# Gated graph network and graph convolution on one core: every turn of h between layers across DRAM, held transfers, and norms in three half-steps

## The chip, the cores and the metric

One core of a Trainium2 chip. A core has five engines, each with its own queue of instructions that it works off in order: PE (TensorE, matrix products into the accumulation banks called PSUM), DVE (VectorE), ACT (ScalarE), POOL (GpSimd), and SP (SyncE, which here only issues transfers). Transfers (DMA) between DRAM and the on-chip memory SBUF are issued from SP and POOL. The metric is the device time of one execution in microseconds (us); lower is better.

## The reference, cut to what matters

There are 16 graphs ("batches") of 1024 nodes with 128 channels. `adj` holds zeros and ones. Two blocks follow each other, each with a layer norm and a relu in front and a residual around it.

```
h = relu(layernorm(x))                       # block 0: gated graph network, 4 layers
for i in range(4):
    m = adj^T @ (h @ weight[i])              # per batch: 1024 x 1024 by 1024 x 128
    r = sigmoid(m @ Wr + h @ Ur + b);  z = sigmoid(m @ Wz + h @ Uz + b)
    n = tanh(m @ Wn + b + r * (h @ Un + b))
    h = (1 - z) * n + z * h
x = x + h * nodemask
h = relu(layernorm(x))                       # block 1: graph convolution, 4 layers
for i in range(4):
    h = relu(adj @ (h @ W[i]) + b[i])
    h = batch_norm over all 16 * 1024 nodes (gamma[i], beta[i])
out = x + h
```

## The kernel before, in words

`exact_path` does the work. Block 0 takes the batches two at a time: stream `sa` has the even batches, `sb` the odd ones. Everything in block 0 is in the layout "channels on the 128 partitions, nodes along the row", except what enters the product with `adj` (`aggregate_rows`, L525), which needs h with nodes on the partitions. So between two layers h has to be turned. The turned h is split into a high part (fp32r, ACT) and a low part (the rest, DVE): `ghw`, two tiles of 128x1024.

The turn is done in two ways. *Across DRAM*: DVE turns blocks of 32x32 (`half_out`, L704), SP stores the half (256 KB) to a scratch tensor `cross_h` (L591), four SP loads of 64 KB bring it back in the other order (`exchange_in`, L598, tile `n_h`), and `split_back` (L852 on ACT, L853 on DVE) makes `ghw`. *On PE*: `features_times` with no weights (L498), eight transposes into PSUM, then L502 on ACT and L503 on DVE. `turned_away` (L828) decides: across, except in the first two half-steps and except for `sb` ahead of its layer 3.

The order is written out in `half_step(one, two)`: the gates of `two` (`gate_step`, L916 on PE, then L928 to L943 on ACT and DVE, one half of 512 nodes after the other), then the product with `adj` of `one` (`agg_step`), for the layer that follows. The next half-step swaps them. A pair of batches takes eight half-steps. This text numbers them by what is multiplied with `adj`:

| step | product with adj | gates | also, before the change |
|---|---|---|---|
| 0 | sb layer 0 | sa layer 0 | `transposes` starts on the new pair |
| 1 | sa layer 1 | sb layer 0 | xmid of the old sa stored |
| 2 | sb layer 1 | sa layer 1 | ymid of the old sa, xmid of the old sb stored |
| 3 | sa layer 2 | sb layer 1 | start: ymid of the old sb, both x of the next pair loaded, adjT of sa stored |
| 4 | sb layer 2 | sa layer 2 | |
| 5 | sa layer 3 | sb layer 2 | start: adjT of sb stored; end: `fetch` for sa |
| 6 | sb layer 3 | sa layer 3 | h of sb turned on PE; rows of the next sa; end: `fetch` for sb |
| 7 | next sa layer 0 | sb layer 3 | rows of the next sb |

Beside this runs the preparation of other work:

- *adj for block 1* (`Feed`, `transposes`): POOL casts a row block to bf16 (L609), SP turns it by a transposing transfer (L610) into the one tile `adjT` (2 MB), and POOL stores that to `adjT_d` (L623). `feed.some(n)` takes n of the sixteen row blocks of a pair.
- *adj of the next batch*: `fetch` (L794) and `stage_rows` (L573) load eight row blocks of 512 KB, four at a time, into `stage`, which is the same memory as `adjT`. POOL rounds each to fp32r (`round_rows`, L578). Each is also looked at, to see that its values are exact: on ACT (`glance`, L587) for blocks 0 to 3, on DVE (`look`, L604) for 4 to 7. Then the next four may be loaded over them.
- *norms*: sums (L651, L652 on DVE), a root and factors (L655 on ACT, L658, L663 on DVE), eight normed blocks (L667 on ACT). Each root brings two table loads on ACT. `xmid_d` and `ymid_d` (512 KB each a batch) hold the residual and the normed input of block 1; POOL stores them. The x of the next pair is loaded by POOL as well (L540).

POOL and SP follow the written order. PE, DVE and ACT are put in order by a planner when the kernel is built, within the data dependences and the `behind(...)` edges, which say only "not ahead of this instruction of the same engine".

Block 1 (from L1177) multiplies again with `adj`, with the blocks loaded from `adjT_d`; the change does not touch it but for the name of one call.

Of the kernel before, what the change touches and what calls it, by code (L numbers as in the profile page):

```python
# [16 lines left out]
P = 128  # L17
# [324 lines left out]
def exact_path(  # L342
# [191 lines left out]
    with ExitStack() as st:  # L534
# [77 lines left out]
        def transposes(batches):  # L612

            for b, rows in batches:
                adjT = turned_tile(f"adjT{b}")
                ahead = transpose_rows(b, rows[0], 0, adjT)
                for j in range(NB):
                    go = ahead
                    if j + 1 < NB:
                        ahead = transpose_rows(b, rows[j + 1], j + 1, adjT)  # L620
                    go()
                    yield j
                nc.gpsimd.dma_start(adjT_d[b].rearrange("k p n -> p k n"), adjT)  # L623

        class Feed:
            jobs, open = iter(()), True

            def some(self, n):
                for _ in range(n):
                    if self.open and next(self.jobs, None) == NB - 1:  # L630
                        self.open = False

        feed, later = Feed(), []

        def soon(b, go):

            later.append(go) if b + 2 < B else go()

# [60 lines left out]
        def blocks_out(src, name):  # L699

            return [half_out(cross_tile(f"t_{name}_{hf}"), src, hf, name) for hf in range(NH)]

        def half_out(t, src, hf, name):
            nc.vector.transpose(by_nodes(t), four_ways(src[:, hf * HALF : (hf + 1) * HALF]))  # L704
            return exchange_out(t, f"{name}_{hf}")

        def cross_tile(name):
            return half_tile(name).bitcast(F32)

        def tail_norm(b, xt, hT, parts=None):  # L710

            for hf in range(NH):
                if parts:
                    pt = by_nodes(parts[hf])
                else:
                    pt = tmp(f"pt_x{b}_{hf}")
                    for q in range(BH):
                        k = hf * BH + q
                        nc.tensor.transpose(pt[:, q * P : (q + 1) * P], hT[:, k * P : (k + 1) * P], ident)
                    pt = four_ways(pt)  # L720
                for q in range(BH):
                    k = hf * BH + q
                    xk = xt[:, k, :].rearrange("p (a c) -> p a c", a=4)
                    mask = maskT[:, b * NB + k : b * NB + k + 1]
                    nc.vector.scalar_tensor_tensor(xk, pt[:, q, :, :], mask, xk, ALU.mult, ALU.add)
            nt = norm_stats(xt, f"mid{b}")
            if b + 1 < B:
                y = work.tile([P, N], F32, tag="h", name=f"y_mid{b}", bufs=7)
            else:
                y = xt.rearrange("p k c -> p (k c)")  # L730
            soon(b, lambda: nc.gpsimd.dma_start(xmid_d[b].rearrange("(k p) c -> p k c", p=P), xt))

            def rest():
                norm_apply(xt, y, nt)
                soon(b, lambda: nc.gpsimd.dma_start(ymid_d[b], y))

            return rest
# [10 lines left out]
        class Stream:  # L748


            def __init__(self, first):
                self.b, self.i, self.tag = first, 0, "AB"[first % 2]
                self.opened, self.across, self.ends, self.stage = None, False, [], None
                self.outs, self.split, self.started = [], [], False

# [32 lines left out]

            def prepare(self):
                self.next_y = work.tile([P, N], F32, tag=f"y{self.tag}", name=f"y_in{self.b + 2}", bufs=1)  # L790
                with behind(self.last_act):
                    norm_blocks(self.next_x, self.next_y, self.next_norm, range(NB))

            def fetch(self):  # L794

                if self.i == 3 and self.b + 2 < B:
                    stage = turned_tile(f"stage{self.b + 2}").bitcast(F32)
                    self.stage = [stage[:, 2 * q : 2 * q + 2, :].rearrange("p a n -> p (a n)") for q in range(4)]
                    stage_rows(self.b + 2, self.stage, range(4))

            def root_ahead(self):
                if self.i == 2 and self.b + 2 < B:
                    with behind(self.last_act):
                        norm_root(self.next_norm, 0, NB)
                        norm_scale(self.next_norm, 0, NB)

            def first_four(self):
                if self.stage:
                    with behind(self.first_act):
                        glance(self.b + 2, self.stage, range(4))  # L810
                    self.rows = round_rows(self.b + 2, self.stage, range(4))
                    stage_rows(self.b + 2, self.stage, range(4, NB))

            def last_four(self):
                if self.stage:
                    self.rows += round_rows(self.b + 2, self.stage, range(4, NB))
                    with behind(self.last_dve):
                        for j in range(4, NB):
                            look(self.b + 2, self.stage[j % 4], j)
                    self.stage = None  # L820

# [6 lines left out]
            def turned_away(self, i):  # L828

                return not written[0] and i < L and not (self is sb and i == 3)  # L830

            def half_away(self, hf):

                if self.turned_away(self.i + 1 - hf):
                    nm = f"{self.b}_{self.i + 1 - hf}"
                    self.outs.append(half_out(cross_tile(f"t_h{nm}_{hf}"), self.new, hf, f"h{nm}"))

# [109 lines left out]

            def ahead(self):

                if self.b + 2 >= B:  # L950
                    return
                if self.i == 2 and self is sa:
                    later.extend((sa.load_ahead, sb.load_ahead))
                if self.i == 3:
                    self.prepare()

            def finish(self):
# [4 lines left out]
                self.b, self.i = self.b + 2, 0  # L962
                ins = self.take() if self.b < B else None
                if not ins:
                    self.ends = [tail_norm(*args)]
                    return
                h_in = self.hT
                outs = blocks_out(args[-1], f"out{args[0]}")
# [7 lines left out]

                later.append(arrive)
                self.ends = [lambda: self.ends.append(lambda: self.ends.append(tail_norm(*args, parts)))]

            def end_step(self, *after):  # L980
                if self.ends:
                    with behind(*after):
                        self.ends.pop(0)()

            def sums_ahead(self, two):

                if self.i == 2 and self.b + 2 < B:
                    self.next_norm = norm_tiles(f"in{self.b + 2}")
                    with behind(two.last_dve):
                        norm_sums(self.next_x, self.next_norm, range(NB))  # L990

        def deliver():
            for go in later:
                go()
            later.clear()

        def half_step(one, two, gated=None, halfway=None):

            feed.open = True
            deliver()  # L1000
            if one is sb and one.i == 0 or not sb.started:
                feed.jobs, sb.started = transposes([(s.b, s.rows) for s in (sa, sb)]), True
            if one.i > 0:
                one.split_step()
            if one.i > 0:
                feed.some(2)
            two.gate_step(0)
            two.half_away(0)
            two.first_four()
            two.root_ahead()  # L1010
            one.split_back(0, two.last_act, two.last_dve)
# [3 lines left out]
            two.gate_step(1, None, one.split)  # L1015
            two.half_away(1)
            if one.i == 0:
                feed.some(1)
# [7 lines left out]
            if halfway:  # L1026
                halfway()
            one.end_step(two.last_act, *one.split)
            two.end_step(two.last_dve, *one.split)
            with behind(*one.split):  # L1030
                two.ahead()
            feed.some(1)
            with behind(*one.split):
                one.sums_ahead(two)
            one.agg_step(1)
            two.finish()
            one.fetch()

        sa, sb = Stream(0), Stream(1)
        every = {getattr(mybir.EngineType, e) for e in ("PE", "DVE", "Activation", "Pool", "SP")}  # L1040
        with tc.tile_pool(name="prep", bufs=1) as prep, tc.manual_schedule(engines=every):
# [101 lines left out]
            sb.agg_rows(range(4, NB))  # L1143
            sa.ahead()

            def looks():
                for j in range(4, NB):
                    first_look(1, j, raw1[j])

            half_step(sa, sb, looks, lambda: turn_layer(prep, w_g, 1))  # L1150
            join_layer(1)
# [4 lines left out]
        with tc.manual_schedule(engines={mybir.EngineType.Pool, mybir.EngineType.SP}):  # L1156
            written[0] = False
            for s in range(2, B // 2 * L):
                half_step(sa, sb)
                half_step(sb, sa)  # L1160
            deliver()
            sb.gate_step(0)
            sb.gate_step(1)
            with tc.issue_after(sb.last_act.ins):
                sa.ends.pop()()
            sb.finish()
# [164 lines left out]
    for b in range(B):  # L1331
# [4 lines left out]
        if waiting:  # L1336
            last = first_weights(*waiting, stats)
            if b == 1:
                with tc.issue_after(last.ins):
                    sb.ends.pop()()  # L1340
        if b == B - 1:
# [117 lines left out]
```

## Time and profile before

| what | us |
|---|---|
| median of 3 runs | 1822.87 |
| the three runs | 1816.81, 1822.87, 1825.02 |
| the profiled execution | 1826.22 |
| its span | 1824.3 |
| PE busy, share of the span | 1772.9, 97% |
| DVE, ACT, POOL busy | 1249.3, 1076.2, 364.4 |

The profile is one execution. The span is from its first to its last recorded instruction; the profiled execution is 1.9 us longer than its span and 3.35 us above the median. Block 0 takes about the first 1200 us of the span. PE's clock is at 9 tenths or more of full speed in all 40 slices.

### The profile page before, as it was taken

What the parts mean: (1) busy time and instruction counts of PE and PEld (TensorE: products, weight loads), DVE (VectorE), ACT (ScalarE), POOL (GpSimd) and SP (SyncE); (2) the same over time, 40 slices, a digit from 0 to 9 for tenths busy, and PEclk for the clock granted to TensorE, in tenths of its full rate; (3) what the DMA queues carried; (4) which work ended last, traced back from release to release, by engine and by line L of the source; (5) the groups of instructions that cost most, each with busy time, mean ns of one, the idle gap of its engine ahead of it and who ended that gap; (6) DMA issues with size and microseconds to landing.
All of it is one profiled execution on the core that took longest, in us unless ns stands there. A gap on an engine that the chain in (4) does not pass through costs nothing.

```text
span 1824.3 us, 22144 instructions
## 1 busy us (share of the span) xinstructions
PE 1772.9 (97%) x6806; PEld 1202.5 (66%) x6806; DVE 1249.3 (68%) x2319; ACT 1076.2 (59%) x1661; POOL 364.4 (20%) x378
## 2 busy tenths in 40 slices
PE   8999999999999999999999999999999999999997
PEld 5565655556555656565655555567778888888886
DVE  7667757767766866776776775676666666666665
ACT  5355546455457465555545545467677768768764
POOL 4223223322322332322232232010100000000010
PEclk9999999999999999999999999999999999999999
DMA  7366676775776677667586577678866666666666
GB/s 257 90 207 209 164 192 214 205 195 185 227 195 187 212 199 202 209 169 205 199 214 182 193 222 210 205 255 302 306 221 222 240 217 244 224 238 231 242 219 256
DMA packets 352447, 390.71 MB, mean 214 GB/s; under 512 B 158540, under 2 KB 231024, under 8 KB 352320
## 3 DMA queue, kind: packets, MB, share of 16 engines
q1 hardware_dynamic: 331568, 314.15, 56.1%
q0 software_dynamic: 20224, 74.80, 11.8%
q8 instruction: 55, 0.90, 0.2%
q14 instruction: 72, 0.59, 0.1%
q10 hardware_dynamic: 528, 0.26, 0.0%
HBM read 262.75 MB, written 92.80 MB: 195 GB/s over the span
## 4 chain that ended last, share of the span: by engine, by line
PE 63%; DVE 13%; DMA 9%; ACT 7%; SPq 4%; issue 4%; POOL 0%; DVEq 0%; ACTq 0%; POOLq 0%
PE pm L525 13%; PE pc_m L525 12%; PE g_r L916 6%; PE pc_g_r L525 6%; PE pc_g_z L525 6%; PE g_z L916 6%; PE hw_c L500 4%; DMA n_h<-cross_h 4%; PE g_xn L916 3%; SPq L598 3%; DVE h L943 2%; PE g_hn L916 2%; DVE low L604 2%; DVE h L942 2%; DMA cross_out<-t_out 1%
## 5 line engine op out<-in xcount | busy, mean ns | idle before, releaser
L525 PE MATMUL pm<-row,ghw 128*128 128x512 f32 x2048 | 514.9, 407 | 15.5 <-DVE ghw L853 15.5
L525 PEld LDWEIGHTS pm<-row,ghw 128*128 128x128 f32 x2048 | 387.0, 190 | 130.5 <-issue 29.7
L525 PE MATMUL pc_m<-wide,chw 128*128 128x512 f32 x1024 | 246.0, 395 | 0.0
L929 DVE SCALAR_TENSOR_TENSOR r<-g_hn,vecs,r 128x512 f32<-128x512 f32 x128 | 95.3, 745 | 180.0 <-ACT r L928 103.2
L525 PEld LDWEIGHTS pc_m<-wide,chw 128*128 128x128 f32 x1024 | 190.5, 188 | 42.3 <-issue 4.3
L609 POOL CAST half<-row 128x1024 bf16<-128x1024 f32 x128 | 138.3, 1090 | 311.0 <-DMA adjT<-half 296.8
L578 POOL CAST row<-stage 128x1024 fp32r<-128x1024 f32 x112 | 129.3, 1156 | 294.7 <-DMA stage<-in_adj_dram 213.1
L525 PE MATMUL pc_g_r<-wide,chw 128*128 128x512 f32 x464 | 187.0, 403 | 0.3 <-ACT chw L502 0.3
L525 PE MATMUL pc_g_z<-wide,chw 128*128 128x512 f32 x464 | 180.9, 390 | 0.0
L891 ACT COPY m<-pm 128x512 f32<-128x512 f32 x128 | 68.5, 587 | 188.7 <-PE pm L525 188.5
L934 ACT ACTIVATE r<-r,vecs 128x512 f32<-128x512 f32 x128 | 92.0, 719 | 145.5 <-DVE r L930 145.5
L1191 DVE CAST wide<-block 128x1024 fp32r<-128x1024 bf16 x160 | 109.9, 692 | 75.2 <-PE pc_m L525 40.0
L1191 DVE CAST wide<-packed 128x1024 fp32r<-128x1024 bf16 x160 | 110.3, 691 | 73.4 <-PE pc_g_z L525 54.2
L916 PE MATMUL g_r<-m,w_mT 128*128 128x512 f32 x256 | 131.5, 595 | 9.4 <-ACT m L891 9.4
L1189 ACT CAST wide<-packed 128x1024 fp32r<-128x1024 bf16 x96 | 100.6, 1048 | 59.3 <-PE pc_m L525 29.8
L935 ACT ACTIVATE z<-g_z,brz 128x512 f32<-128x512 f32 x128 | 86.9, 679 | 81.0 <-PE g_z L916 80.8
L1189 ACT CAST wide<-block 128x1024 fp32r<-128x1024 bf16 x96 | 100.7, 1049 | 57.2 <-PE pc_g_z L525 27.7
L916 PE MATMUL g_xn<-m,w_mT 128*128 128x512 f32 x256 | 130.7, 592 | 0.0
L916 PE MATMUL g_z<-m,w_mT 128*128 128x512 f32 x256 | 130.7, 592 | 0.0
L941 DVE TENSOR_TENSOR h<-h,r 128x512 f32<-128x512 f32 x96 | 75.3, 785 | 69.7 <-ACT r L934 69.6
L1239 DVE BATCH_NORM_STATS2 stats<-feat 128x6 f32<-128x512 f32 x128 | 84.1, 686 | 46.9 <-ACT feat L1238 45.8
L928 ACT ACTIVATE r<-g_r,brz 128x512 f32<-128x512 f32 x128 | 87.8, 686 | 43.7 <-PE g_r L916 43.3
(185 smaller groups left out, 2793.8 us busy)
## 6 DMA issues: line engine op xcount, KB each, us to landing
packed<-adjT_d SPq DMA_DIRECT2D x256, 256.0 KB, 5.7
block<-adjT_d SPq DMA_DIRECT2D x256, 256.0 KB, 4.6
stage<-in_adj_dram SPq DMA_DIRECT2D x120, 512.0 KB, 5.1
adjT_d<-adjT POOLq DMA_DIRECT2D x16, 2048.0 KB, 9.2
cross_h<-t_h SPq DMA_DIRECT2D x74, 256.0 KB, 2.3
n_h<-cross_h SPq DMA_DIRECT2D x296, 64.0 KB, 2.1
xmid_d<-x POOLq DMA_DIRECT2D x16, 512.0 KB, 5.1
y<-ymid_d POOLq DMA_DIRECT2D x16, 512.0 KB, 6.0
```

Of the source, the lines that this page charges most:

```text
L525: nc.tensor.matmul(pm[hf], hw[s][:, j * P : (j + 1) * P], rows[j][:, hf * HALF : (hf + 1) * HALF], start=(j == 0 and s == 0), stop=(j == N ...
L578: nc.gpsimd.tensor_copy(t, stage[j % 4])
L609: nc.gpsimd.tensor_copy(t, row.bitcast(F32))
L916: nc.tensor.matmul(po, wT[:, i, g * C : (g + 1) * C], rhs, start=start, stop=stop)
L928: self.first_act = nc.scalar.activation(r, pr, AF.Sigmoid, bias=brz[:, 3 * i : 3 * i + 1])
L929: nc.vector.scalar_tensor_tensor(r, phn, b_hn(i), r, ALU.add, ALU.mult)
L934: nc.scalar.activation(r, r, AF.Tanh, bias=b_in(i))
L935: self.last_act = nc.scalar.activation(z, pz, AF.Sigmoid, bias=brz[:, 3 * i + 1 : 3 * i + 2])
L941: nc.vector.tensor_sub(ho, hin, r)
L1189: nc.scalar.copy(r, t)
L1191: nc.vector.tensor_copy(r, t)
L1239: nc.vector.bn_stats(stats[:, b * NH + hf, :], dst)
```

## The change

1. `turned_away` no longer leaves out `sb` ahead of layer 3: eight turns go across DRAM that were done on PE. `self.last_dve` becomes the DVE turn of the half.
2. The large POOL transfers (adjT, xmid, ymid, x) are no longer issued at the start or end of a half-step. They are issued in its middle, on POOL behind a small copy `pace` that reads a column of the first half of the new h. adjT of sa goes out in step 2, that of sb in step 5. `x` of sa is loaded in step 3, of sb in step 4.
3. Each norm is spread over the ends ("gap") of three half-steps, written down in an agenda: sums, then root and factors, then blocks. Before, the root of the next pair's norm was taken between the two halves of the gates, and the norm of the finished pair was done in two places.
4. `fetch` moves from the end of a half-step to the start of the next; for sa it stands on SP behind the return of sb's h. Blocks 4 to 7 are loaded in `last_four`, not `first_four`. ACT looks at block 0 behind the first sigmoid of the first half of the gates, at 1 to 3 behind that of the second half. Blocks 4 to 7 of `sb` are looked at on ACT in step 0, no longer on DVE in step 7.
5. In the first half-step all eight row blocks of sa's `adjT` are turned.

```diff
+            def store(self):
+                if self.full and not self.stored:
+                    self.stored = next(self.jobs) == NB
...
-                return not written[0] and i < L and not (self is sb and i == 3)
+                return not written[0] and i < L
...
+                    at(n + 2, "gap", sums)
+                    at(n + 3, "mid", lambda: store_xmid(b, xt))
+                    at(n + 3, "gap", lambda: norm_factors(end["norm"]))
+                    at(n + 4, "gap", blocks)
+                    at(n + 5, "mid", lambda: store_ymid(b, end["y"]))
+                if self.b + 2 < B:
+                    at(n + 5, "mid", self.next_load)
+                    at(n + 5, "gap", self.next_sums)
+                    at(n + 6, "gap", self.next_factors)
+                    at(n + 7, "gap", self.next_blocks)
...
             def first_four(self):
                 if self.stage:
                     with behind(self.first_act):
-                        glance(self.b + 2, self.stage, range(4))
+                        glance(self.b + 2, self.stage, range(1))
                     self.rows = round_rows(self.b + 2, self.stage, range(4))
-                    stage_rows(self.b + 2, self.stage, range(4, NB))
 
             def last_four(self):
                 if self.stage:
+                    with behind(self.first_act):
+                        glance(self.b + 2, self.stage, range(1, 4))
+                    stage_rows(self.b + 2, self.stage, range(4, NB))
                     self.rows += round_rows(self.b + 2, self.stage, range(4, NB))
+                    b, stage, self.stage = self.b + 2, self.stage, None
+                    if self is sb:
+
+                        at(clock[0] + 1, "late", lambda: glance(b, stage, range(4, NB)))
+                        return
                     with behind(self.last_dve):
...
         def half_step(one, two, gated=None, halfway=None):
 
-            feed.open = True
-            deliver()
-            if one is sb and one.i == 0 or not sb.started:
-                feed.jobs, sb.started = transposes([(s.b, s.rows) for s in (sa, sb)]), True
+            feed.next_step()
+            one.split = []
+            if one.i == 0:
+                two.fetch()
+            due("ins")
+            if one is sb and one.i == 0 or written[0] and one is sa:
+                feed.jobs = transposes([(s.b, s.rows) for s in (sa, sb)])
             if one.i > 0:
                 one.split_step()
-            if one.i > 0:
+                two.fetch()
                 feed.some(2)
             two.gate_step(0)
             two.half_away(0)
             two.first_four()
-            two.root_ahead()
+            if feed.full or (clock[0], "mid") in agenda:
+
+                pace = small.tile([P, 1], F32, tag="pace", name=f"pace{clock[0]}")
+                nc.gpsimd.tensor_copy(pace, two.new[:, :1])
+                feed.store()
+                due("mid")
             one.split_back(0, two.last_act, two.last_dve)
             one.split_back(1, two.last_act, two.last_dve)
             if one.i > 0:
                 feed.some(1)
             two.gate_step(1, None, one.split)
             two.half_away(1)
+            with behind(two.first_act):
+                due("late")
...
-            one.end_step(two.last_act, *one.split)
-            two.end_step(two.last_dve, *one.split)
-            with behind(*one.split):
-                two.ahead()
-            feed.some(1)
-            with behind(*one.split):
-                one.sums_ahead(two)
+            with behind(two.last_act, two.last_dve, *one.split):
+                due("gap")
+            feed.some(NB if written[0] and one is sa else 1)
             one.agg_step(1)
             two.finish()
-            one.fetch()
+            clock[0] += 1
```

## The prediction

> **What bounds the kernel now.** I read the page first (is one engine full?), then PE's timeline for one pair of batches (where is it not?), then the chain of waits back from each gap.
>
> ```profile
> span 1824.3 us, 22144 instructions
> PE 1772.9 (97%) x6806; PEld 1202.5 (66%) x6806; DVE 1249.3 (68%) x2319; ACT 1076.2 (59%) x1661; POOL 364.4 (20%) x378
> ```
>
> PE is the bound. So a change can gain only what PE does needlessly, and PE's gaps. PE's timeline of one pair (start, us, engine, line, tiles; the bracket is the idle time ahead and what ended it):
>
> ```profile
> 684.42 7.11 PE L525 MATMUL pm<-row,ghw 128*128 128x512 f32 x30 [0.49 <-DVE ghw L853]
> ...
> 701.27 7.84 PE L525 MATMUL pm<-row,ghw 128*128 128x512 f32 x32
> ...
> 718.85 7.85 PE L525 MATMUL pm<-row,ghw 128*128 128x512 f32 x32
> 726.54 0.60 PE L498 MATMUL hw_g<-ident,h 128*128 128x128 f32 x4
> 728.28 0.66 PE L498 MATMUL hw_g<-ident,h 128*128 128x128 f32 x4 [1.15 <-DVE h L943]
> ...
> 755.83 1.12 PE L916 MATMUL g_z<-h,w_hhT 128*128 128x512 f32 x2 [0.73 <-ACT z L935]
> ...
> 804.47 1.12 PE L916 MATMUL g_r<-m,w_mT 128*128 128x512 f32 x2 [1.60 <-ACT m L891]
> ...
> 832.41 7.78 PE L525 MATMUL pm<-row,ghw 128*128 128x512 f32 x26 [1.88 <-DVE ghw L853]
> ```
>
> An undisturbed half-step is 718.85 - 701.27 = 17.58 us; eight are 140.64. This pair took 832.41 - 684.42 = 147.99. The same starts over seven pairs (129.62 to 1162.59 us) give 147.57 a pair, so 6.93 us a pair is lost. I split it by the steps in which it falls, averaged over the seven pairs: 2.31 in steps 6 and 7 (the turn on PE, its wait for h, a wait for a z bank), 1.36 in steps 0 and 1 (the wait for m), 3.26 in steps 2 and 3 (the wait for ghw). Removing all of it would be worth about 7 x 6.93 + 3 (the last pair's turn step, 20.62 us) = 52 us: no reading of this change ends below about 1771.
>
> The chain of waits behind the last gap, and POOL's timeline just ahead of it:
>
> ```profile
> 820.45 0.79 SPq L598
> 821.28 7.73 DMA n_h<-cross_h
> 829.20 0.48 issue
> 829.69 0.69 ACT r L928
> ...
> 831.07 0.68 DVE h L943
> 831.75 0.61 DVE ghw L853
> 832.41 2.76 PE pm L525 x6
> ```
>
> ```profile
> 819.28 0.56 POOL L735 DMA_DIRECT2D ymid_d<-y_mid  x1 [12.54 <-ACT y_mid L667]
> 819.84 1.77 POOL L540 DMA_DIRECT2D x<-in_x_dram  x2
> 821.60 0.89 POOL L623 DMA_DIRECT2D adjT_d<-adjT  x1
> ```
>
> The last 64 KB of the returning h took 7.73 us, where the page gives 2.1 as the median. POOL had issued 3.5 MB in the 3 us around it. ACT waits in its queue with the copy of that half; the sigmoid of the gates stands behind it, DVE behind the sigmoid, and DVE's low part of the *first* half, which PE wants, behind that.
>
> **The change part by part.**
>
> *The turn (part 1).* Eight turns leave PE: 8 transposes x 145 ns (12.8 us busy over 88) = 1.16 us each, 9.3 us, all on the path, as PE is the bound. Their copies (L502 0.60 and L503 0.69 us, twice) give way to L852 0.61 and L853 0.78, twice: nothing. Added for each turn: two DVE turns of 0.70 us, two stores and eight loads on SP (some 4.9 us of issue). When is it back? DVE's h is done at 728.24, and at about 726.8 without the doubled L942 and L943 of 1.41 us beside POOL's casts, which go elsewhere. Then 0.7 turn, 2.3 out, 1.7 issue, 2.1 back: 733.6; 1.4 for the split: 735.0. PE wants it at 726.5 + 10.3 (gates) = 736.8. So the cover is 1.8 us for the first four blocks, 3.6 more for the rest; without it, it costs what it is late. What was waiting around the turn (2.31 - 1.16 = 1.15 us a pair) I do not count as gained: the z bank is held up by DVE, where sa's four looks (4.5 us) stay, and the staged rows come later (below).
>
> *The held transfers (part 2).* The adjT store of sa leaves from the middle of step 2, at about 813.5 (first half of h at 812.5, `pace`, issue 0.89), with 0.5 MB of xmid; the profile's landings of 8.1 to 12.2 us put its end at 822 to 826. The returning second half is then in by about 825 and split by 827, wanted at 829.5 + 3.6. Ends late next: the planned order of DVE, some tenths. I count 2.4 of the 3.26 us a pair: 7 x 2.4 = 16.8 us. Queued behind `pace` on POOL, up to 9 us of a half-step: the stores and loads themselves and the casts of the last two row blocks (L609, 1.09 us each), whose transposing transfers on SP slip with them; adjT is wanted two half-steps on. The trace has no POOL copy of one column; by its DMA issues it is 0.5 to 0.9 us, or nearly nothing by its 128 elements, off the path in steps 1 to 5 either way. POOL is busy 20%.
>
> Here a rule of the Trainium skill speaks against the change. "DMA: Bandwidth & Descriptors", section "Queues, rings and completion order", says that each DMA engine goes round between the queues that have work, a packet at a time. Two busy queues (SP's, POOL's) would then slow a 2.1 us load to some 4.2 (an estimate from the page), and the half would land at 825.5, ahead of 829: no wait to remove, and the sum of the change would be the 9.3 of the turn alone. The trace has 7.73, and 6.68 at the other store (712.88 us, step 5). I take the measurement, 16.8, and keep the other as a rival. The rule also says that the bytes don't go away: the store now meets the *second* half's way out (817.2 us). At 8 us instead of 2.3 this comes back at about 829, still ahead of 833.1.
>
> *The norms (part 3).* The same instructions in other places. Two table loads and a root (1.28 + 0.30 + 1.28 us) leave the middle of ACT's gates and go behind them, where ACT waits for PE (188.5 us at L891). Sums of 8 x (0.26 + 0.16) = 3.4 us come in DVE's gap; x is issued some 8 us ahead of them and lands in 7.3. If it is late, DVE stands, and the next gate's r with it: up to 2 us in steps 3 and 4, which have no wait now; unlike it may gain the 1.36 us of steps 0 and 1. Bounds -9.5 to +10 us over the pairs; I take zero.
>
> *Rows and looks (part 4).* sa's fetch is issued at 719.86 now, when the store of sb's adjT (711.75) has landed. That store moves to about 717.1, landing at 726 to 728, and the fetch stands on SP behind the eight loads of h, whose last go at 731.6: 11.8 us later. But blocks 4 to 7 are now issued at 732.5 to 737.3 because ACT's looks and a busy row tile (735.89, wait for PE) hold them; with rows landing from 735 they go at 737 to 741.7, 4.4 later, land by 747, and DVE's looks end at 748.5, now 749.0. So it is just covered. For sb, four looks of 1.21 us leave DVE and 4 x (1.05 + 0.19) come to ACT in step 0, beside PE's 17.58. Zero, with a bound of +8 us a pair where the cover fails. Part 5: once, some 0.
>
> *Sum:* 9.3 + 16.8 = 26.1. The profiled execution's 1826.2 becomes 1800.1; it stood 3.4 above the median, so 1797.
>
> **The rivals.**
>
> *More goes than I count* (25%): the store at 711.75 also made h late for the turn (ACT waited for n_h until 719.66, then the table load, 721.59), so the 1.15 a pair around the turn goes too (9 us), and the steps 0 and 1 are planned anew (9.5): 1797 - 18.5 = 1778. For it: these waits hang on the same transfers. Against: sa's looks stay on DVE.
>
> *The hold only moves the collision* (14%): the second half or x is met instead. Only the turn remains: 1822.9 - 9.3 = 1813.5. For it: DMA is busy 68 to 69% throughout these stages.
>
> *Slower: the staged rows come late* (10%). Place: SP, the fetch behind the return of h, in step 6. If blocks 4 to 7 slip by 8 of the 11.8 us, sa's looks stand at the head of DVE's queue, sb's gates of step 7 (L929 at 751.87) behind them, and PE behind a bank. It has no slack there (0.73 us wait now), so about 7 us a pair: 49 - 26 = 23 slower, 1846. It decides from a slip of about 5 us, where the loss (some 4 us a pair) equals the 26 gained. Against: the 4.4 worked out above, which DVE's later end of looks absorbs.
>
> *It does nothing measurable* (3%): PE waits as long for h across as it spent on the turn, and the planner's order keeps the gaps: 1821.
>
> **How the numbers follow.** The case of the sum has 48%, 1788 to 1806. A measurement of this kernel can tell about 0.5% from no change: below 1813.8 is faster, above 1832.0 slower. Faster: 48 + 25 + half of 14 = 80%. Same: 7 + 3 + 1 (the mild end of late rows) = 11%. Slower: 9%. The range goes from 1773 (most of the second case) to 1822 (the third and the fifth); left out are the slower case and a tail of the second.
>
> **What would show it.** Right: 24 records of L498 `hw_g` instead of 88; `cross_h` issued 90 times, not 74; adjT_d issued in steps 2 and 5 beside a finished first half; no n_h landing of over 6 us on the chain in step 3; steps 2 and 3 together at 35.2 to 36; pairs at about 144. Wrong: gaps of PE behind `ghw` in step 6 (the turn is late), behind `row` in step 0 or 7, or `DMA stage` ended DVE or ACT waits of several us in steps 6 and 7 (the rows are late); or n_h landings over 6 us elsewhere (the collision moved).

## The result and the profile after

Over twelve runs of each, the changed kernel takes 1811.6 us (1809.0 to 1816.0) where the kernel before took 1828.0 (1816.8 to 1832.8): a ratio of 0.9915, with a 95% interval of 0.9897 to 0.9933, or 15.5 us (the medians lie 16.4 apart). The forecast was 26 us, and a time of 1797. Direction and range held; the runs below show that the sum behind them did not. One of its two terms had the wrong sign, and the other came out larger than forecast, partly in other steps.

The page after (span, then busy time of each engine):

```profile
span 1808.8 us, 22303 instructions
PE 1767.1 (98%) x6742; PEld 1192.1 (66%) x6742; DVE 1282.7 (71%) x2307; ACT 1106.7 (61%) x1717; POOL 389.2 (22%) x417
```

PE does 64 matmuls fewer, as forecast, and DVE is busy 33 us longer. Of that, 22 us are one group of the gates (128x512, two inputs in SBUF): 128 instructions of 918 ns, before 743. No term of the sum had that. The gaps of PE's timeline that answer to those shown of before (`L906` is now the low part, `L969` the gates):

```profile
240.37 7.14 PE L525 MATMUL pm<-row,ghw 128*128 128x512 f32 x30 [0.94 <-DVE ghw L906]
...
290.95 1.03 PE L525 MATMUL pm<-row,ghw 128*128 128x512 f32 x2
293.40 6.87 PE L525 MATMUL pm<-row,ghw 128*128 128x512 f32 x29 [1.42 <-DVE ghw L906]
...
1110.73 1.13 PE L969 MATMUL g_r<-h,w_hhT 128*128 128x512 f32 x2 [1.76 <-ACT r L981]
...
1116.21 8.73 PE L525 MATMUL pm<-row,ghw 128*128 128x512 f32 x30 [3.13 <-DVE ghw L906]
```

Step 3 (240 us) still waits for the low part, less than before. Step 6 (293 us) waits for it too: that is the turn that was taken off PE. The last pair's step 3 (1110 to 1116 us) is new, and worse than any pair before. To compare kernels, I took from PE's timeline the time from the start of one step's product to that of the next, less the undisturbed 17.58 us. Counted so, a step's stretch holds the gates of the step behind it: the turn on PE, ahead of the product of step 6, falls under step 5. The columns are the mean over six full pairs (step 2 to step 1 of the next pair) of one profiled execution, in us; then the sum of steps 2 to 5 of the last pair, and the ratio to the kernel before. The names of the kernels are those of the experiments below. The prediction's 6.93 us a pair is 7.33 here, over slightly other pairs:

```
kernel         step 2   step 3   step 4   steps 5-7  steps 0-1   pair   last pair   ratio
before          0.02     3.39     0.00      2.50       1.41      7.33      5.06
after           0.04     1.27     0.13      1.68       1.45      4.57      8.59     0.9915
turn_alone      0.01     4.02     0.00      3.50       3.10     10.63      2.14     1.0107
no_turn         0.04     1.21     0.22      0.88       0.95      3.30     11.52     0.9857
no_pace         1.09     1.41     0.61      3.18       1.57      7.86      4.36     1.0024
nt_no_pace      0.69     1.16     0.89      2.71       0.85      6.31     11.47     0.9990
casts_later     0.07     1.33     0.04      0.55       1.44      3.42      9.56     0.9861
nt_y            0.04     0.79     0.28      0.89       0.82      2.81      7.00     0.9846
nt_y_low        0.00     0.30     0.00      0.85       0.89      2.03      4.54     0.9821
nt_y_second     1.61     1.14     1.41      1.21       1.05      6.42      8.01     0.9989
nt_y_lowfree    0.01    -0.01    -0.01      0.86       1.11      1.96      2.34     0.9778
ac_all          0.08     0.78     0.06      0.05       1.45      2.42      1.02     0.9793
ac_free         0.01     0.00    -0.01     -0.02       1.43      1.41     -0.01     0.9763
```

The waits that the change was about, in the list of waits (who waited for whom: us in total, times, longest). Before:

```profile
ACT ghw L852 <- DMA n_h<-cross_h: 43.8, 22, 3.7
...
DVE ghw L853 <- ACT ghw L852: 22.2, 15, 2.4
...
PE pm L525 <- DVE ghw L853: 15.5, 7, 3.2
```

After:

```profile
POOL pace L1052 <- DVE h L996: 186.6, 26, 16.1
...
PE pm L525 <- DVE ghw L906: 17.1, 14, 3.1
...
ACT ghw L905 <- DMA n_h<-cross_h: 12.6, 11, 3.6
```

ACT waits 12.6 us for the returning h, not 43.8: the transfers are out of its way. Of the 360 loads of h none takes over 6 us now (the longest 5.55); before, 21 of 296 did. Yet PE waits for `ghw` as long as before, twice as often: 7 us of it in step 6, 9 in step 3, of which 3.1 in the last pair. Outside the last pair, what is late is now mostly the instruction of DVE that works on the data, as the experiments show.

### The profile page after: what moved, and what is told of

Read it like the earlier page. It is cut to its first block, busy times and chain, and to the rows that moved or that the text cites. A ratio compares the mean times of both kernels' runs of the same rounds, so it can differ in the third digit from the quotient of the medians.

```text
span 1808.8 us, 22303 instructions
## 1 busy us (share of the span) xinstructions
PE 1767.1 (98%) x6742; PEld 1192.1 (66%) x6742; DVE 1282.7 (71%) x2307; ACT 1106.7 (61%) x1717; POOL 389.2 (22%) x417
## 3 DMA queue, kind: packets, MB, share of 16 engines
q0 software_dynamic: 20224, 74.80, 11.4%
## 4 chain that ended last, share of the span: by engine, by line
PE 77%; DVE 8%; DMA 6%; ACT 4%; issue 3%; SPq 2%; DVEq 0%; POOL 0%; ACTq 0%
PE pm L525 20%; PE pc_m L525 13%; PE g_z L969 8%; PE g_r L969 8%; PE pc_g_z L525 6%; PE pc_g_r L525 6%; PE hw_c L500 4%; PE g_xn L969 4%; PE g_hn L969 4%; DMA stage<-in_adj_dram 2%; DMA cross_h<-t_h 2%; DVE ghw L906 2%; SPq L598 1%; DVE h L994 1%; DMA n_h<-cross_h 1%
## 5 line engine op out<-in xcount | busy, mean ns | idle before, releaser
L609 POOL CAST half<-row 128x1024 bf16<-128x1024 f32 x128 | 152.0, 1196 | 316.9 <-DMA adjT<-half 301.8
L982 DVE SCALAR_TENSOR_TENSOR r<-g_hn,vecs,r 128x512 f32<-128x512 f32 x128 | 95.5, 746 | 154.7 <-ACT r L981 111.4
L994 DVE TENSOR_TENSOR h<-h,r 128x512 f32<-128x512 f32 x96 | 88.9, 926 | 68.0 <-ACT r L987 67.9
L969 PE MATMUL g_r<-m,w_mT 128*128 128x512 f32 x256 | 131.5, 595 | 3.8 <-ACT m L944 3.8
L969 PE MATMUL g_xn<-m,w_mT 128*128 128x512 f32 x256 | 131.5, 595 | 3.1 <-ACT m L944 2.2
L969 PE MATMUL g_z<-m,w_mT 128*128 128x512 f32 x256 | 130.7, 592 | 0.0
L995 DVE TENSOR_TENSOR h<-h,z 128x512 f32<-128x512 f32 x128 | 117.0, 918 | 6.9 <-DVE h L994 0.9
```

Of the source, the lines that this page charges most:

```text
L609: nc.gpsimd.tensor_copy(t, row.bitcast(F32))
L969: nc.tensor.matmul(po, wT[:, i, g * C : (g + 1) * C], rhs, start=start, stop=stop)
L982: nc.vector.scalar_tensor_tensor(r, phn, b_hn(i), r, ALU.add, ALU.mult)
L994: nc.vector.tensor_sub(ho, hin, r)
L995: nc.vector.tensor_mul(ho, ho, z)
```

## The experiments

Two theories stood at the start. *Sum*: the turn gains its PE time, the hold the rest. *Rival*: the PE time of the turn came back as a wait. The first four runs take the parts away one at a time.

**The turn alone.** To the kernel before:

```diff
-                return not written[0] and i < L and not (self is sb and i == 3)
+                return not written[0] and i < L
```

> The kernel before with one edit: sb's h ahead of layer 3 is turned across DRAM too. Theory 'the turn is a gain by itself' (the step of the sum): PE loses 8 x 1.16 us, steps 6 and 7 together lose 1.2 us a pair less than the 2.31 they lose now, about 0.995 of the kernel before. Rival 'the turn needs the rest of the change': here fetch stands on SP ahead of the return of h (blocks 0 to 3 and, in first_four, 4 to 7 behind it on the same queue), so PE waits for ghw in step 6 by 3 us or more a pair; no gain or slower, 1.00 to 1.02. The first needs n_h of step 6 issued by about 733 on the scale of the profile before, the second shows it behind stage on SP.

Measured: 1847.5 us, ratio 1.0107 (1.0071 to 1.0144). Slower by some 19 us, as the rival said. SP's part of the timeline in step 6:

```profile
279.31 11.12 SPq L591 DMA_DIRECT2D cross_h<-t_h  x2
...
290.53 1.83 SPq L573 DMA_DIRECT2D stage<-in_adj_dram  x4
...
292.47 6.44 SPq L598 DMA_DIRECT2D n_h<-cross_h  x8
```

The second half of h leaves at 290.10, the four row loads stand behind it on SP and the way back behind those. But h was late already: with the store of adjT not held, ACT waited 2.97 us for the half that returned ahead of it (until 282.18), and the gates behind it. So the trace shows two causes, and the order on SP need not be the larger: no_pace below, with the new order on SP and no hold, still loses 3.18 us in steps 5 to 7, against 3.50 here. Steps 0 and 1 lose 3.10, which I did not follow further.

**Everything but the turn.** To the changed kernel:

```diff
-                return not written[0] and i < L
+                return not written[0] and i < L and not (self is sb and i == 3)
```

> The changed kernel with the exception put back: sb's h ahead of layer 3 is turned on PE. If the turn's share of the gain is what the step table gives (7.7 us over eight turns), this is about 1819, 0.9955 of before. Theory 'the turn is worth its PE time' says steps 6 and 7 lose 2.3 a pair again instead of 1.7. Rival 'the removed PE time came back as a wait for ghw': the difference to the changed kernel is under 4 us, and the whole gain is the hold, the norms and the looks.

Measured: 1803.2 us, ratio 0.9857 (0.9821 to 0.9893). Neither: taking the turn out makes the changed kernel *faster*, by 8.4 us in the medians. The groups of the turn on PE, before and here:

```profile
L498 PE MATMUL hw_g<-ident,h 128*128 128x128 f32 x88 | 12.8, 276 | 4.4 <-DVE h L943 4.2 <-ACT w_mT L488 0.2
```

```profile
L498 PE MATMUL hw_g<-ident,h 128*128 128x128 f32 x88 | 11.8, 273 | 0.2 <-ACT w_mT L488 0.2
```

Here the turn no longer waits for h (idle time ahead 0.2 us, before 4.4). It costs its 0.88 us a pair and nothing around it. Across DRAM it costs 1.68 in steps 5 to 7, and 0.5 more in steps 0 and 1, where PE's planned order is another. In each pair but the first of every kernel with all turns across, PE's first matmul behind the product of step 0 needs ACT's copy of that product and waits 0.45 us; with the turn on PE another comes first and there is no wait. The changed kernel, then no_turn:

```profile
190.76 1.13 PE L969 MATMUL g_xn<-m,w_mT 128*128 128x512 f32 x2 [0.45 <-ACT m L944]
```

```profile
189.35 1.02 PE L969 MATMUL g_r<-h_in,w_hhT 128*128 128x512 f32 x2
```

Only in the last pair is the turn across the better one: 0.03 in step 5, on PE 3.71.

**The hold.** To the changed kernel:

```diff
-                pace = small.tile([P, 1], F32, tag="pace", name=f"pace{clock[0]}")
-                nc.gpsimd.tensor_copy(pace, two.new[:, :1])
```

> The changed kernel without the small POOL copy that holds the large transfers: they stay at the same place of POOL's order, but go as soon as their own data is there, up to some 7 to 15 us earlier (POOL waited 186.6 us in 26 such copies). Theory 'the hold pays': the transfers meet the return of the other stream's h at the start of the half-step, ghw waits grow again in steps 3 to 5, towards the 3.26 us a pair of before, 10 to 20 us slower than the changed kernel, 0.997 to 1.002 of before. Rival 'the hold only moves the collision, the gain is the place in the order': within 4 us of the changed kernel, 0.99 to 0.994; step 3 of the last pair, where the held 2.5 MB now meet the second half, gets better by up to 5 us.

Measured: 1832.3 us, ratio 1.0024 (1.0008 to 1.0039): without the hold all is lost, 20 us. The last pair is better by 4.2, as the second theory said. Its list of waits:

```profile
POOL adjT_d L623 <- DMA adjT<-half: 114.9, 16, 11.7
...
PE pm L525 <- DVE ghw L906: 31.9, 29, 2.9
...
ACT ghw L905 <- DMA n_h<-cross_h: 23.6, 15, 3.4
```

The stores now go as soon as adjT is there, and PE waits twice as long for `ghw`. But step 3 stays near its 1.27 (1.41); the losses come in steps 2, 4, and 5 to 7. The landings of h say the same: loads of over 4 us ahead of step 3's product were 13 before, 1 here, 3 in the changed kernel; ahead of step 5's, 15 before, 13 here, none in the changed kernel. So the wait in step 3 went with the rest of the change, the transfers' new place among it, and the copy keeps the way clear in the other steps. POOL's casts, which the copy holds as well, are not how it gains: without it DVE's low part is faster (mean 0.92 us, with it 1.05).

The same edit on no_turn:

> The kernel of no_turn without the hold (pace copy). With the turn across, taking the hold away cost 20 us. It leaves the norms in three half-steps, the looks and the fetch in their new places as what differs from the kernel before, and the place of the large transfers in POOL's order. Theory 'the hold is nearly the whole gain': 0.998 to 1.002 of before, steps 2 to 4 lose 3 us a pair again. Rival 'hold and turn across belong together (only the turn across needs the hold)': 0.986 to 0.990, as no_turn. Rival 'the norms and looks bring a part': 0.992 to 0.997.

Measured: 1822.3 us, ratio 0.9990 (0.9977 to 1.0002). With either turn nothing measurable is left without the hold. Here too step 3 is at 1.16, not back at 3.39, and steps 2, 4, and 5 to 7 lose more than in no_turn. So what else changed (the transfers' new place, norms in three half-steps, looks, fetch) sums to nothing that can be measured without the hold; it does not follow that each of them is nothing.

**POOL's casts in step 6.** DVE and POOL of the changed kernel in that step, start and duration:

```profile
289.05 1.41 DVE L995 TENSOR_TENSOR h<-h,z 128x512 f32<-128x512 f32 x1
290.38 0.74 DVE L982 SCALAR_TENSOR_TENSOR r<-g_hn,vecs,r 128x512 f32<-128x512 f32 x1
291.04 0.86 DVE L996 TENSOR_TENSOR h<-h,r 128x512 f32<-128x512 f32 x1
291.83 2.96 DVE L906 TENSOR_TENSOR ghw<-n_h,ghw 128x512 fp32r<-128x512 f32 x2
```

```profile
288.59 7.10 POOL L578 CAST row<-stage 128x1024 fp32r<-128x1024 f32 x5 [14.02 <-DMA stage<-in_adj_dram]
```

ACT began the high part at 286.99, four microseconds ahead of PE's need. The low part (L906) stands in DVE's queue behind the gates' h, and while POOL casts, DVE's instructions with two inputs in SBUF take longer than their 0.69 us: L995 1.41, L996 0.86, the two of L906 1.52 each. L982, with an input in PSUM, stays at 0.74. In the whole trace, 272 instructions of L994 to L996 and L906 had no POOL cast beside them, and none took over 0.70 us; the 37 with one beside them throughout took 0.68 to 1.53. The Trainium skill, "SBUF — State Buffer", section "Who interferes with whom", says that a DVE instruction with two SBUF inputs contends with a GpSimd instruction that reads SBUF. The rows agree, and both sides are slowed: POOL's casts, 1.04 us elsewhere, take 1.42 here (7.10 for five). The edit:

```diff
             def first_four(self):
...
-                    self.rows = round_rows(self.b + 2, self.stage, range(4))
+            def casts(self, low=None):
+                if self.stage:
+                    if low is not None:
+                        pace = small.tile([P, 1], F32, tag="pace", name=f"pace_r{self.b}")
+                        nc.gpsimd.tensor_copy(pace, low[:, :1].bitcast(F32))
+                    self.rows = round_rows(self.b + 2, self.stage, range(4))
...
+            low = one.hw[1] if one.outs else None
             one.split_back(1, two.last_act, two.last_dve)
+            two.casts(low)
```

> The changed kernel, but POOL's casts of blocks 0 to 3 of sa's new rows stand behind the low part of the first half of sb's h in step 6 (a small POOL copy of one of its columns ahead of them). Theory 'POOL's casts double DVE's instructions': in step 6 L995 and L906 take 0.69 again instead of 1.41 and 1.53, and PE's wait for ghw there (1.0 to 2.9 us a pair) falls by 1.4; 7 us faster than the changed kernel if the rows, which come some 3 us later, are still in time. Rival 'h is late from DRAM': the wait stays, as its data is not there. A third outcome: the wait moves to the rows in step 7 or 0, no change of time.

Measured: 1804.4 us, ratio 0.9861 (0.9826 to 0.9896), 7.2 us faster than the changed kernel. The same stretch now (L1001 is L995, L912 is L906):

```profile
287.13 0.69 DVE L1001 TENSOR_TENSOR h<-h,z 128x512 f32<-128x512 f32 x1
287.74 0.74 DVE L988 SCALAR_TENSOR_TENSOR r<-g_hn,vecs,r 128x512 f32<-128x512 f32 x1
288.41 0.68 DVE L1002 TENSOR_TENSOR h<-h,r 128x512 f32<-128x512 f32 x1
289.00 1.29 DVE L912 TENSOR_TENSOR ghw<-n_h,ghw 128x512 fp32r<-128x512 f32 x2
```

Steps 5 to 7 lose 0.55 us, not 1.68, and the rows, though later, are in time. The casts in DVE's way were the larger part of that wait.

**The last pair.** There the held transfers get company. POOL in step 2 of the last pair, in no_turn:

```profile
1082.11 0.19 POOL L1052 COPY pace<-h 128x1 f32<-128x1 f32 x1 [6.63 <-DVE h L996]
1082.62 0.89 POOL L623 DMA_DIRECT2D adjT_d<-adjT  x1 [0.32 <-issue]
1083.50 0.89 POOL L743 DMA_DIRECT2D xmid_d<-x  x1
1084.38 2.77 POOL L609 CAST half<-row 128x1024 bf16<-128x1024 f32 x2
1087.10 0.57 POOL L1289 DMA_DIRECT2D y<-ymid_d  x1
```

Block 1's first load, 512 KB, goes out 4 us behind 2.5 MB. The edit puts that load behind the last adjT store of block 0 on POOL:

```diff
-                nc.gpsimd.dma_start(adjT_d[b].rearrange("k p n -> p k n"), adjT)
+                last_store[0] = nc.gpsimd.dma_start(adjT_d[b].rearrange("k p n -> p k n"), adjT)
...
-        nc.gpsimd.dma_start(yt, ymid_d[b])
+        with tc.issue_after(last_store[0].ins):
+            nc.gpsimd.dma_start(yt, ymid_d[b])
```

> The kernel of no_turn (turn of sb's h ahead of layer 3 on PE again), and block 1's loads of ymid stand on POOL behind the last adjT store of block 0. In step 3 of the last pair no_turn loses 7.35 us, in the other pairs 0.5 to 1.8; there the first of these loads (512 KB) is issued at 1087.10, 4 us behind the held 2.5 MB, ahead of h's way back. Theory 'the load on top of the held burst makes h late': step 3 of the last pair falls to about 19, some 5 to 6 us in all, 0.982 to 0.984 of before. Rival 'the last pair is late for another cause (the planner's order with block 1's work in it)': step 3 stays near 24.9, no change of time.

Measured: 1796.0 us, ratio 0.9846 (0.9821 to 0.9871). The last pair's step 3 loses 1.06 us, not 7.35; of that 1.3 comes back in its step 5 (5.02, was 3.71). So the theory holds for the step. The ratio is only 0.0011 below that of no_turn, with intervals that overlap, and misses the 0.982 to 0.984 expected.

**DVE's order.** In the changed kernel `last_dve` became the turn of the new half, and the low part of the other stream's h must stand behind it. To nt_y:

```diff
-                    out, self.last_dve = half_out(cross_tile(f"t_h{nm}_{hf}"), self.new, hf, f"h{nm}")
+                    out, _ = half_out(cross_tile(f"t_h{nm}_{hf}"), self.new, hf, f"h{nm}")
```

> The kernel of nt_y, and the low part of the returned half no longer waits on DVE for the turn of the new half (half_away leaves last_dve with the last h instruction). Theory 'what is left in steps 3 and 4 is DVE's order': the low part starts 0.7 us earlier, PE's wait for ghw in step 3 falls by 0.6 to 0.7 in each pair that has one, 4 us in all. Rival 'the planner puts another instruction there': the wait stays, under 1 us in all. The turn that it passes leaves 0.7 us later, which should cost nothing, as h's way back has some 4 us to spare for the second half.

Measured: 1791.0 us, ratio 0.9821 (0.9796 to 0.9845), 5.1 us faster than nt_y on the same chip. Step 3 loses 0.30, not 0.79, step 4 nothing. With no edge at all on the low part:

```diff
-                    with behind(*after):
-                        self.split = [
-                            nc.scalar.copy(hi, back),
-                            nc.vector.tensor_sub(lo, back, hi.bitcast(F32)),
-                        ]
+                    with behind(*after[:1]):
+                        high = nc.scalar.copy(hi, back)
+                    self.split = [high, nc.vector.tensor_sub(lo, back, hi.bitcast(F32))]
```

> The kernel of nt_y with no edge of DVE's order on the low part at all (in nt_y it stands behind the turn of the new half, in nt_y_low behind the last h of that half). Theory 'the earlier the better for PE's wait': steps 3 and 4 lose no more than in nt_y_low, 0.981 to 0.983 of before. Rival 'the edge keeps DVE from standing still': the planner sets the low part ahead of the gates' h where h's way back is still under way on the chip, DVE waits in its queue with h behind it, and single steps lose 2 to 5 us: 0.985 to 0.995.

Measured: 1786.6 us, ratio 0.9778 (0.9757 to 0.9799), better than I expected of either side: steps 2 to 4 lose nothing in any pair. Against nt_y_low, which ran on another chip, the table gives 2.6 us (6 x 0.07 + 2.20); the rest of the 4.4 between the medians it does not show.

**ACT's order.** The other way to free the first half's low part, on nt_y:

```diff
-            one.split_back(1, two.last_act, two.last_dve)
...
             two.gate_step(1, None, one.split)
             two.half_away(1)
+            one.split_back(1, two.last_act, two.last_dve)
```

> The kernel of nt_y, and both parts of the second returned half come behind the second half of the gates, not between. In step 3 ACT's copy of the second half waits for its transfer (up to 1.7 us) with the gates' tanh behind it, DVE's h behind that and the first half's low part behind h. Theory 'ACT's queue hands the late transfer on': the wait in step 3 goes, 1.0 us a pair, 6 us in all. Rival 'then the second half itself is late': PE needs it 3.64 us into the product, the gates' second half ends later than that, and PE waits in every step for it: 1 to 3 us a step, 50 us or more slower.

Measured: 1822.5 us, ratio 0.9989 (0.9976 to 1.0001), 26 us slower than nt_y. The rival was right in kind, and half its size: PE stops inside the product for the second half's low part, and steps 2, 3 and 4 lose 1.1 to 1.6 us each.

**The turn again, with the way clear.** All turns across, with the edits of casts_later, nt_y and nt_y_low:

> The changed kernel (all turns across DRAM) with three edits together: POOL's casts of sa's first rows behind the low part (casts_later), block 1's first loads of ymid behind the last adjT store (nt_y), the low part not behind DVE's turn (nt_y_low). Theory 'the turn across loses only by what stands in its way': step 6 is then free, steps 5 to 7 lose 0.2 a pair instead of 0.86 with the turn on PE, the last pair's 3.7 is gone, and 0.7 a pair in step 0 remains: 8 x 0.6 + 3 - 7 x 0.7 = 3 us faster than nt_y_low, 0.980 to 0.981 of before. Rival 'the turn across costs elsewhere': the step 0 price of 0.7 and late rows outweigh it, 2 to 6 us slower than nt_y_low, 0.983 to 0.986.

Measured: 1788.8 us, ratio 0.9793 (0.9771 to 0.9815), a little better than the theory, and a second time beside the last kernel:

> The kernel of ac_all once more, beside ac_free on the same chip, since the differences between these kernels are under 0.3%: 0.979 to 0.980 of before.

1789.5 us, 0.9794 (0.9770 to 0.9817). With the edit of nt_y_lowfree in place of that of nt_y_low:

> All turns across DRAM, the casts behind the low part, block 1's loads late, and no edge of DVE's order on the low part: ac_all with nt_y_lowfree's edit instead. In nt_y_lowfree steps 2 to 5 lose nothing, the turn on PE 0.86 a pair and 2.3 in the last, steps 0 and 1 0.7 to 1.5. If the edits add, steps 5 to 7 lose nothing here and step 0 keeps 0.7: 8 x 0.86 + 1.5 - 7 x 0.7 = 3.5 us faster than nt_y_lowfree, 0.976 of before. Rival 'in step 6 DVE then stands still for the late h': 0.979 to 0.982, no better than ac_all.

Measured: 1783.7 us, ratio 0.9763 (0.9740 to 0.9787), the fastest of all, and 5.8 us faster than ac_all_again on the same chip. Its page and its list of waits:

```profile
span 1780.0 us, 22318 instructions
PE 1757.9 (99%) x6742; PEld 1193.6 (67%) x6742; DVE 1250.7 (70%) x2307; ACT 1107.4 (62%) x1717; POOL 392.2 (22%) x424
```

```profile
PEld pm L525 <- DVE ghw L913: 0.2, 1, 0.2
```

PE no longer waits for `ghw`. What is left is 1.43 us a pair in steps 0 and 1. Against nt_y_lowfree, the turn across, with the casts behind the low part, is now worth 6 x 0.55 + 2.35 = 5.7 us in the table. The two times, not taken side by side, are 2.9 us apart, with intervals of the ratios that overlap: that it is a gain now rests on the table, one profiled execution of each.

## Why the prediction was right or wrong

That the time fell into the range was in part luck: two terms were off in opposite directions. Of the signs named ahead of time, the counts held, and no load of h takes over 6 us; steps 2 and 3 together came out at 36.5 us, not 35.2 to 36, the pairs at 145.2, not 144. One sign of being wrong appeared: PE waits behind `ghw` in step 6.

*The turn: forecast -9.3 us, measured +8.4 by the medians, +10.6 by the ratios.* The step that failed is "when is it back?". The sum counted DVE's turn, the way out and back, and "1.4 for the split", as if the split began when the data came. The data was in time (ACT began the high part at 286.99, against a need at 290.95). The low part was not: it stood in DVE's queue behind the gates' h, and POOL's casts, which my own text had seen double L942 and L943, doubled it. I said those casts "go elsewhere" and did not ask where: they went beside the low part. casts_later shows that this was most of the wait: 1.13 of 1.68 us a pair. Nor had the sum the 0.7 us of step 0, of which 0.45 is PE's wait for the copy of a product (no_turn, above).

*What stood around the turn: forecast to stay, 1.15 a pair; it went.* no_turn has steps 5 to 7 at 0.88, all of it the turn itself; without the hold (nt_no_pace) they are at 2.71. So it hung on the transfers that the copy holds, as the case "More goes than I count" had it (it named the store of sb's adjT).

*The hold: forecast -16.8 us; it is worth 20 to 24.* no_pace gives 20 us; nt_no_pace, on another chip than no_turn, 19 by the medians and 24 by the ratios. The size was about right, the path was not. The gain was placed in step 3, and step 3 did lose 2.1 us a pair less, near the 2.4 of the sum; but it keeps that without the copy (1.41 and 1.16). Taking the copy out costs in steps 2, 4 and 5 to 7: the 20 us are the price of these transfers in the new order, not only what the old order lost. Which part of the change freed step 3 no run takes apart.

The weighing of the 7.73 us row against the rule came out on the side of the measurement: by the estimate of 4.2 us there was nothing to gain. That estimate took a packet of each queue as the same amount of data. In the profile before, POOL's queue moved 74.80 MB in 20224 packets (3.7 KB each) and SP's 314.15 MB in 331568 (0.95 KB), so turns by the packet need not be equal shares. Whether that makes up the 7.73 us, no run shows. The way out did slow, as forecast, but less: the longest store of a half of h took 5.80 us (before 4.30), not 8.

*The last pair: not foreseen.* The same burst, plus 0.5 MB of block 1, cost 5.5 us more than before in one step (7.44 against 1.98). The case "The hold only moves the collision" is true there, in the changed kernel there alone.

*Norms, looks, rows: forecast zero; not measured by themselves.* nt_no_pace (0.9990, 0.9977 to 1.0002) has them together with the transfers' new place, which may cancel them in part. Late rows, the case that ends slower, show in turn_alone: ACT waits 26.0 us there for staged rows, in the changed kernel 9.6, in no_pace 8.1. So it was not the hold that kept them out but the rest of the change, the fetch and the looks in their new places among it.

So the 15.5 us are about 26 from the hold and what came with it (no_turn, 0.9857), less 10.6 for the turn (0.9915 - 0.9857 = 0.0058 of 1828). The sum missed by 10.6 us as well: the turn was off by 20, and the hold and what came with it gave 9 back.

Open: why the planner sets another order in step 0 in the kernels with all turns across (20.86 against 20.15 us). The place of each norm, the looks and the fetch were not tried singly.

## What to carry to other kernels

When a transfer comes off the critical path, look next at the in-order queue of the engine that takes its data in: here the bytes were in time and the last subtraction was not. A large store that is not needed soon can be held by a one-column copy that reads what must go first; it costs POOL, busy 22% of the span, 0.3 us (39 copies of 294 ns) and was worth 20 in this order. And work that is moved off one engine is judged by the engine that receives it: the same turn across DRAM cost 8 to 11 us behind a crowded queue and gained 3 to 6, by the table, once the queue was clear.

## What was not expected of the hardware

A small load beside a burst of large transfers suffered more than the 4.2 us estimated ahead: 64 KB in 7.73 us where 2.1 is the median, with 3.5 MB issued around it. Half a megabyte more behind 2.5 MB turned a loss of 1.06 us in one step into 7.35. DVE and POOL slow *each other*: DVE's instructions with two SBUF inputs went from 0.69 to as much as 1.5 us, POOL's casts from 1.04 to 1.42.
